# A two-layer fp32 kernel on one core: the first pair's projections as whole products, weight sums on VectorE, and a reordered layer 0 and tail

## The chip, the cores and the metric

The kernel runs on one core of one Trainium2 chip. Its engines run side by side, each in the order of its own queue, and wait for each other through semaphores: TensorE (PE: matrix products), VectorE (DVE), ScalarE (ACT), GpSimd (POOL) and SyncE (SP, which here only issues DMAs). The metric is the device time of one execution in microseconds (us), as the median of several runs. A profile is one further execution, recorded instruction by instruction.

## The reference, cut to what matters

Eight batches of 128 rows and 512 columns go through two layers, all in fp32. Both add their result to x.

```python
# layer 0: a per-batch 512x512 weight, then a feed-forward with 2 of 8 LoRA experts
c    = einsum('bsi,boi->bso', x, weight[adapter_ids])
wts  = softmax(top_k(einsum('bsd,ed->bse', c, gate_w), 2))
x    = x + einsum('bsd,od->bso', c, base_w) + base_b + 2 * lora(c, wts)
# layer 1: attention over a paged cache, then 16 of 64 small experts
q, k, v = x @ Wq.T, x @ Wk.T, x @ Wv.T        # 32 query heads, 8 key/value heads of 128
q, k = rope(rmsnorm(q)), rope(rmsnorm(k))
keys, values = concat(cache[pages], k), concat(cache[pages], v)     # 512 + 128 rows
o    = softmax(mask(q @ keys.T * SCALE)) @ values
x    = x + expert_ffn(o @ Wo.T)
```

## The kernel before, in words

Every instruction is placed by hand: the order of the calls in the program is the order of each engine's queue. Nothing is reordered by a scheduler. Tiles come from pools with a fixed number of buffers, and an instruction that writes a reused buffer waits until the old content has been read.

**Layer 0** (L347 to L626) loops over t = 0 to 7, one batch each. In one turn PE does: the first half of the adapter product (L470), the transpose of the low-rank values of batch t-1 (`ltp`, L528), the second half of the adapter, the experts' product of t-1 (`bp`, L534), the transposes of the finished rows of t-2 (`x1tp`, L553), then for batch t the gate and low-rank product (`gl`, L487, written into the adapter's bank `cp`) and the base product (L492). The adapter's result is copied to `cT` by DVE (L479). The top-2 choice is a chain of some dozen small DVE instructions in `l0_base` (L498 to L516), ended by `low`; one of them (L505) needs `lg`, whose upper part POOL fills with a large number, the sentinel (L497), and one (L510) needs an exponential from ACT (`ex`, L507). `l0_experts` adds up the row (L536), takes its largest value and a power of two from it (`up`, L540 to L545), ACT scales the row by it (L544), POOL forms `eps` (L546), and SP writes the row to memory. `l0_turn` then transposes it and ACT copies it to `xo` (L555), the input of layer 1.

**The projections** use a form of Strassen's and Winograd's scheme. Two batches form a pair. Both the pair's input and the weights are split into halves, and 7 products of half size (2 matmuls each) take the place of 8. `PRODUCTS` (L239) lists which sums of inputs and of weights each one multiplies; seven sums' places lie beside the data in `xo` (second index 0 to 6) and in the weight tile `wqkv` (likewise). The sums of the inputs (`sums_x`, 4 subtractions or additions of 256 columns) and of the weights (`sums_q`, 4 subtractions of 768 columns) are done on POOL. The results are put together by additions on DVE (L261), 7 for a pair and a weight tile. `project(k, j, products)` does the named products of pair k with weight tile j. Products 1, 3, 4 and 6 go to PSUM bank "q", and 2, 5 and 7 to bank "kv". In layer 0 `x1tp` uses bank "q" as well (for t-2 up to 5), and `ltp` uses bank "kv" (for t-1 up to 6).

**A unit** u is one batch with one key/value head (4 query heads): batch and head group follow from u, and 64 units make up layer 1. Pair 0 gives units 0 to 3, with weight tile 0 for units 0 and 2 and tile 1 for 1 and 3. `norms(u)` squares and sums the 5 heads on ACT and takes the root on POOL (`rs`, L295). `rotate(u)` applies the rotary embedding with 6 DVE instructions (L307 to L325; L321 needs `rs`) and leaves `ca`. Units 0 to 2 then have their heads transposed on PE (`transpose_qk`, `tq`, L339) and copied by ACT to `qkT`; later units go through an exchange by DMA (`blocks_qk`, `exchange_out`, `exchange_in`, `heads_qk`).

**The main loop** calls `iteration(u)` for u = 0 to 66. It runs, for each of 4 heads: two score products on PE (L768, L771); on DVE the scale, mask and smallest value (L781, giving `low`); the exponential on ACT (L792); the reciprocal of its sum on DVE (`den`, L797); the scaling on POOL (L798); and 32x32 block transposes on DVE (L803). Between the heads lie the output products of unit u-3 (L869) and the projections of a later pair (`slots`). At the end come norms and rotate for unit u+3 and the value products of unit u-2 (L847). Scores have two double banks, so the scores of head h+2 wait for L781 of head h. `gather` fetches 16 key pages of 32 KB for each batch through SP (`kt`), `gather_v` the values through POOL (`vt`).

The weight tiles live in two buffers. For each of the 3 later quarters of the heads they are loaded anew (`load_q`, 1.5 MB each, at the end of units 8 and 10, 24 and 26, 40 and 42), and their sums follow on POOL at the end of units 9 to 12, 25 to 28 and 41 to 44 (L1017).

Of the kernel before, what the change touches and what calls it, by code (L numbers as in the profile page):

```python
# [16 lines left out]
P = 128  # L17
B = 8
# [39 lines left out]
def adaln_ffn_kernel(  # L58
# [97 lines left out]

    def sums_q(g, first):

        w = wq_t[g]
        if first:  # L160
            nc.gpsimd.tensor_tensor(w[:, 5], w[:, 3], w[:, 1], ALU.subtract)
            nc.gpsimd.tensor_tensor(w[:, 1], w[:, 1], w[:, 0], ALU.subtract)
        else:
            nc.gpsimd.tensor_tensor(w[:, 4], w[:, 3], w[:, 1], ALU.subtract)
            nc.gpsimd.tensor_tensor(w[:, 6], w[:, 2], w[:, 4], ALU.subtract)

# [82 lines left out]
    def project(k, j, products):  # L249
# [3 lines left out]
        for i in products:  # L253
# [79 lines left out]

    def transpose_qk(u):
# [7 lines left out]
        qkT = pj.tile([P, NH, S], F32, tag="qkT", name=f"qkT_{u}", bufs=2)  # L342
        nc.scalar.copy(qkT.rearrange("p h s -> p (h s)"), t[:, : NH * S])
        qkT_t[u] = qkT


    with ExitStack() as l0:  # L347
# [35 lines left out]
        for b in (5, 6, 7):  # L383
            wt_home[b] = wp.tile([P, NC, DM], F32, tag="wo", name=f"wt_{b}", bufs=GH + 1)
        wt_home[4] = w0p.tile([P, NC, DM], F32, name="wt_4")
# [74 lines left out]

        state, cp_t, cT_t, lowT_t = {}, {}, {}, {}

        def l0_adapter(b, first):

            xT, wt, xb = loaded[b]
            if first:
                cp_t[b] = banks(f"cp_{b}")
            for o in range(0, NC // 2) if first else range(NC // 2, NC):
                for c in range(NC):
# [7 lines left out]
            if not first:  # L477
                cT_t[b] = p2.tile([P, NC, S], F32, tag="cT", name=f"cT_{b}")
                nc.vector.tensor_copy(cT_t[b].rearrange("p c s -> p (c s)"), cp_t[b][:, :DM])  # L479

        def l0_base(b):
# [13 lines left out]

            lg = sm.tile([P, E0 + 8], F32, tag="lg", name=f"lg_{b}")
            nc.gpsimd.memset(lg[:, E0:], BIG)  # L497
            nc.vector.tensor_copy(lg[:, :E0], gl[:, :E0])  # L498
# [62 lines left out]
        for t in range(B):  # L561
# [6 lines left out]
            if t + 2 < B:  # L568
                l0_load_x(t + 2)
            if t >= 1:  # L570
                l0_experts(t - 1)
                if t in (3, 4):
                    load_q(t - 3, nc.gpsimd)
            if 2 <= t <= 5:
# [6 lines left out]
            if t == 5:  # L581
                project(0, 0, (6, 7))
            if t == 6:
                project(0, 0, (3,))
                norms(0)
            if t == 7:
                project(0, 1, (6, 7))
            l0_base(t)
# [4 lines left out]
            if t in (3, 6):  # L593
                gather_v(t // 3 - 1, 0, LC)
            if t in (3, 5, 7):
                sums_x((t - 3) // 2)
            if t in (5, 7):
                make_tables(t // 7)
            if t in (4, 5):
                sums_q(t - 4, True)  # L600
                sums_q(t - 4, False)
            if t == 4:
                project(0, 0, (1, 2))
            if t == 5:
                project(0, 0, (4, 5))
            if t == 6:
                project(0, 1, (1, 2))
                rotate(0)
            if t == 7:
                transpose_qk(0)  # L610
                project(0, 1, (4, 5))
        for g in range(GH):
            load_o(g, nc.gpsimd)
        l0_turn_low(B - 1)
        project(0, 1, (3,))
        norms(1)
        l0_experts(B - 1)
        l0_turn(B - 2)
        rotate(1)
        norms(2)  # L620
        project(1, 0, (1, 2))
        l0_turn(B - 1)
        transpose_qk(1)
        rotate(2)
        project(1, 0, (6, 7))
        sums_x(B // 2 - 1)  # L626

# [103 lines left out]
    with ExitStack() as l1:  # L731
# [99 lines left out]
        def heads_qk(u):  # L831

            qkT = pj.tile([P, NH, S], F32, tag="qkT", name=f"qkT_{u}", bufs=2)
            nc.scalar.copy(
# [98 lines left out]
        def iteration(u):  # L933
# [76 lines left out]
            if on(u + 3):  # L1010
# [178 lines left out]
```

## Time and profile before

| what | value |
|---|---|
| median of 3 runs | 1287.82 us |
| lowest, highest | 1286.24, 1293.43 us |
| the profiled execution | 1288.46 us |
| its span, first to last instruction | 1286.7 us |
| PE busy | 1238.4 us, 96% of the span |
| DVE busy | 924.8 us, 72% |
| POOL busy | 609.3 us, 47% |
| ACT busy | 496.6 us, 39% |
| mean granted PE clock | 0.986 |
| first score product of unit 0 | 131.75 us after the start |
| first score product of unit 3 | 177.02 us |

In the views, a line of the list of instructions gives the start in us, the length, the engine, the source line, the operation, what it writes and reads, and in brackets how long the engine had been idle before it and what ended that idle time. A line of stages gives the stretch, its length, then the busy us of each engine with the number of instructions, the granted PE clock (1.00 is full), the share of the time in which the DMA engines were busy, and GB/s. An fp32 matmul stands as two records. PE runs faster than it looks busy: neighbouring records overlap a little, so lengths of work are best taken from start to start.

### The profile page before, as it was taken

Reading aid. Unit: us, or ns where it says so; the run is one execution under the profiler, and the core shown is the slowest. Engines: PE = TensorE matmul, PEld = TensorE weight load, DVE = VectorE, ACT = ScalarE, POOL = GpSimd, SP = SyncE. Lnnn points to the kernel's source line nnn. Section 1 sums busy time; section 2 is a strip of 40 time slices with the busy share of each in tenths; the row PEclk is TensorE's granted clock in tenths of the full one; section 3 lists DMA queues with packets and bytes.
Section 4 is the critical chain, followed back from the end, with each engine's and each line's share of the span. In section 5 each row is a group of like instructions: output and inputs, shape, how many; then the busy total and the mean of one; then the engine's idle time right before and its main releaser. Section 6 shows DMA issues by size and latency. Waiting matters only on the chain.

```text
span 1286.7 us, 15903 instructions
## 1 busy us (share of the span) xinstructions
PE 1238.4 (96%) x3835; PEld 654.1 (51%) x3835; DVE 924.8 (72%) x2049; ACT 496.6 (39%) x1437; POOL 609.3 (47%) x683
## 2 busy tenths in 40 slices
PE   9888899998999999999999999989999999999998
PEld 7655445554545545544455555544555555545544
DVE  3745887778987777778877777788877777767522
ACT  0222444433444444443444444343444444343210
POOL 2645454456654444456644444465544444443100
PEclk9989899999999999999999999999999999999999
DMA  8823287787887887788877877887878777887512
GB/s 292 277 68 110 86 240 243 246 257 245 263 260 234 266 248 252 246 278 265 276 243 246 275 242 247 281 261 251 273 245 266 244 236 245 272 250 233 181 65 89
DMA packets 211297, 298.99 MB, mean 232 GB/s; under 512 B 84035, under 2 KB 121284, under 8 KB 211204
## 3 DMA queue, kind: packets, MB, share of 16 engines
q1 hardware_dynamic: 180740, 207.83, 52.0%
q10 hardware_dynamic: 18960, 52.21, 12.2%
q0 software_dynamic: 11504, 37.94, 8.7%
q8 instruction: 31, 0.51, 0.2%
q14 instruction: 62, 0.51, 0.1%
HBM read 183.54 MB, written 114.36 MB: 232 GB/s over the span
## 4 chain that ended last, share of the span: by engine, by line
PE 68%; DVE 7%; DMA 6%; ACT 4%; POOL 2%; issue 2%; ACTq 0%; SPq 0%; DVEq 0%; POOLq 0%
PE p L258 16%; PE o L847 16%; PE y L869 14%; PE s L768 14%; PE s L771 4%; DMA px<-pb 3%; PE op L1086 2%; PE fz L680 2%; DMA qkb<-px 2%; ACT sq L289 2%; DVE ca L321 2%; DVE sa L321 2%; DMA kt<-in_kc 1%; POOL rs L295 1%; ACT p L792 1%
## 5 line engine op out<-in xcount | busy, mean ns | idle before, releaser
L798 POOL TENSOR_SCALAR p<-p,den 128x640 f32<-128x640 f32 x256 | 204.5, 799 | 438.0 <-DVE den L797 438.0
L792 ACT ACTIVATE p<-p,low 128x640 f32<-128x640 f32 x256 | 212.0, 828 | 461.3 <-DVE den L797 278.4
L258 PE MATMUL p<-wqkv,xo 128*128 128x384 f32 x896 | 327.2, 495 | 10.3 <-ACT xo L555 9.1
L781 DVE CUSTOM_DVE_ANT_0 p<-s,mask,rs 128x640 f32<-128x640 f32 x256 | 223.7, 879 | 115.3 <-PE s L771 112.6
L768 PE MATMUL s<-kt,qkT 128*128 128x512 f32 x512 | 267.1, 604 | 23.4 <-DVE low L781 16.5
L869 PE MATMUL y<-wo,oT 128*128 128x512 f32 x512 | 262.9, 598 | 3.2 <-ACT oT L858 3.2
L258 PEld LDWEIGHTS p<-wqkv,xo 128*128 128x128 f32 x896 | 172.4, 194 | 166.1 <-issue 81.6
L847 PE MATMUL o<-pT,vt 128*128 128x512 f32 x512 | 230.2, 592 | 0.0
L803 DVE STREAM_TRANSPOSE pb<-p 128x640 f32<-128x640 f32 x256 | 211.3, 825 | 16.2 <-POOL p L798 16.2
L771 PEld LDWEIGHTS s<-qkT 128*128 128x128 f32 x512 | 98.5, 192 | 124.8 <-issue 124.8
L768 PEld LDWEIGHTS s<-kt,qkT 128*128 128x128 f32 x512 | 96.2, 192 | 125.5 <-issue 53.6
L847 PEld LDWEIGHTS o<-pT,vt 128*128 128x128 f32 x512 | 97.3, 190 | 110.3 <-issue 94.9
L203 POOL DMA_INDIRECT vt<-in_vc,vrow x128 | 134.4, 1050 | 38.7 <-issue 28.0
L289 ACT ACTIVATE sq<-c 128x128 f32<-128x128 f32 x320 | 98.8, 309 | 10.5 <-DVE c L261 2.5
L295 POOL TENSOR_TENSOR rs<-ss,mhalf 128x5 f32<-128x5 f32 x64 | 98.1, 1533 | 5.3
L771 PE MATMUL s<-qkT 128*128 128x128 f32 x512 | 99.4, 276 | 0.0
L858 ACT COPY oT<-o 128x512 f32<-128x512 f32 x64 | 37.5, 586 | 138.5 <-PE o L847 133.9
L261 DVE TENSOR_TENSOR c<-c,p 128x384 f32<-128x384 f32 x96 | 51.9, 541 | 44.7 <-PE p L258 44.6
L869 PEld LDWEIGHTS y<-wo,oT 128*128 128x128 f32 x512 | 78.8, 193 | 8.6 <-issue 4.3
L321 DVE SCALAR_TENSOR_TENSOR ca<-c,rs,tab 128x128 f32<-128x128 f32 x64 | 42.6, 665 | 51.0 <-POOL rs L295 51.0
L847 PE MATMUL o<-pT,vn 128*128 128x512 f32 x128 | 65.4, 592 | 0.0
L289 ACT ACTIVATION_READ_ACCUMULATOR sq<-c 128x1 f32 x320 | 59.7, 187 | 0.0
(170 smaller groups left out, 1146.8 us busy)
## 6 DMA issues: line engine op xcount, KB each, us to landing
pT<-px SPq DMA_DIRECT2D x64, 1280.0 KB, 7.4
px<-pb SPq DMA_DIRECT2D x122, 400.0 KB, 5.4
px<-pb ACTq DMA_DIRECT2D x122, 400.0 KB, 5.2
qkb<-px SPq DMA_DIRECT2D x61, 320.0 KB, 3.5
kt<-in_kc SPq DMA_DIRECT2D x512, 32.0 KB, 4.7
wqkv<-in_wqkv POOLq DMA_DIRECT2D x8, 1536.0 KB, 11.4
wo<-in_wo POOLq DMA_DIRECT2D x8, 1024.0 KB, 7.5
yd<-ya SPq DMA_DIRECT2D x24, 256.0 KB, 2.0
```

The lines of the kernel that those rows point to most:

```text
L203: nc.gpsimd.indirect_dma_start(out=kv_t[step][1][:, c, :], out_offset=None, in_=vc, in_offset=bass.IndirectOffsetOnAxis(ap=vrow[:, hf, at ...
L258: nc.tensor.matmul(out=ps, lhsT=xo[:, pr, x, c, :], rhs=w[:, c, :], start=(c == 0), stop=(c == 1))
L289: nc.scalar.activation(sq, cs[:, at : at + D], AF.Square, accum_out=ss[:, h : h + 1])
L295: nc.gpsimd.tensor_tensor(rs, ss, mhalf, ALU.pow)
L768: nc.tensor.matmul(out=s[:, :L], lhsT=qkT[:, h, :], rhs=kt[:, :, g % GH, :], start=True, stop=True)
L771: nc.tensor.matmul(out=s[:, L:NK], lhsT=qkT[:, h, :], rhs=qkT[:, REP, :], start=True, stop=True)
L781: nc.vector.tensor_tensor_reduce(out=p, in0=s_t.pop((u, h))[:, :NK], in1=mask_t[st], scale=rs_t[u][:, h : h + 1], scalar=BIG, op0=ALU.add, ...
L792: nc.scalar.activation(p, p, AF.Exp, bias=low, scale=-1.0, accum_out=den)
L798: nc.gpsimd.tensor_scalar(p_t[u, h], p_t[u, h], den, 1.0, ALU.mult, ALU.mult)
L803: nc.vector.transpose(pb_t[u][:, :, h * w : (h + 1) * w].rearrange("p i (j a) -> p j i a", a=32), p_t.pop((u, h)).rearrange("p (j i a) -> ...
L847: nc.tensor.matmul(out=o, lhsT=vt[:, c, j * D : (j + 1) * D] if c < LC else vn_t.pop(u), rhs=pT[:, c], start=(c == 0), stop=(c == LC),)
L869: nc.tensor.matmul(out=y_t[st], lhsT=oT_t[u][:, h, :], rhs=wo_t[g][:, h, :], start=(h == 0 and j == 0), stop=(h == REP - 1 and j == GH - 1),)
```

## The change

1. **Pair 0 in whole products.** A new function `project_first(j, r, c)` computes one quarter of unit 2r+j directly: 4 matmuls of 384 columns that accumulate in one bank ("kv" for c = 1, "q" for c = 0), and one ACT copy. Eight calls, spread over t = 4 to 7 and the tail, take the place of the 14 products of `project(0, 0, ...)` and `project(0, 1, ...)`. They read only the plain halves of input and weights, so pair 0 needs no sums.
2. **Weight sums on DVE.** `sums_q(g, *tees)` does single named sums with `nc.vector`, 8 in layer 0, its tail and units 0 and 1, and 8 in each later reload: two inside head 1 of units 10 and 12 (mod 16), one at the end of these units, and one inside head 1 of units 11 and 13.
3. **Layer 0.** `cT` is copied by ACT. The `lg` tile and its sentinel come at the start of the turn. `l0_experts(t-1)` moves behind the gathers, `l0_turn(t-2)` and a projection.
4. **Tail.** norms and rotate of units 1 to 3 and the transposes of unit 2 are placed before the main loop; unit 2's heads go to the buffer of the last adapter weight. `sums_x` of pair 3 moves to unit 3, and that of pair 0 to unit 5.

```diff
+    def sums_q(g, *tees):
         w = wq_t[g]
-        if first:
-            nc.gpsimd.tensor_tensor(w[:, 5], w[:, 3], w[:, 1], ALU.subtract)
-            nc.gpsimd.tensor_tensor(w[:, 1], w[:, 1], w[:, 0], ALU.subtract)
-        else:
-            nc.gpsimd.tensor_tensor(w[:, 4], w[:, 3], w[:, 1], ALU.subtract)
-            nc.gpsimd.tensor_tensor(w[:, 6], w[:, 2], w[:, 4], ALU.subtract)
+        for t in tees:
+            to, x, y = {3: (5, 3, 1), 1: (1, 1, 0), 2: (4, 3, 1), 4: (6, 2, 4)}[t]
+            nc.vector.tensor_tensor(w[:, to], w[:, x], w[:, y], ALU.subtract)
...
+    def project_first(j, r, c):
+        u = 2 * r + j
+        if u not in c_t:
+            c_t[u] = pj.tile([P, 2 * HW], F32, tag=f"c{r}", name=f"c{r}_0_{j}", bufs=2)
+        ps = bank("kv" if c else "q", f"p_0_{j}_{r}{c}")[:, :HW]
+        for i in range(4):
+            x = i // 2
+            w = wq_t[j][:, 2 * x + c].rearrange("p (c n) -> p c n", c=2)
+            nc.tensor.matmul(out=ps, lhsT=xo[:, 0, 2 * r + x, i % 2, :], rhs=w[:, i % 2, :],
+                             start=(i == 0), stop=(i == 3))
+        nc.scalar.copy(c_t[u][:, c * HW : (c + 1) * HW], ps)
...
             if first:
                 cp_t[b] = banks(f"cp_{b}")
+                lg_t[b] = sm.tile([P, E0 + 8], F32, tag="lg", name=f"lg_{b}")
+                nc.gpsimd.memset(lg_t[b][:, E0:], BIG)
...
-                nc.vector.tensor_copy(cT_t[b].rearrange("p c s -> p (c s)"), cp_t[b][:, :DM])
+                nc.scalar.copy(cT_t[b].rearrange("p c s -> p (c s)"), cp_t[b][:, :DM])
...
-            if t >= 1:
-                l0_experts(t - 1)
-                if t in (3, 4):
-                    load_q(t - 3, nc.gpsimd)
+            if t in (3, 4):
+                load_q(t - 3, nc.gpsimd)
...
             if t == 5:
-                project(0, 0, (6, 7))
+                project_first(0, 0, 1)
+                norms(0)
             if t == 6:
-                project(0, 0, (3,))
-                norms(0)
+                project_first(0, 1, 0)
             if t == 7:
-                project(0, 1, (6, 7))
+                project_first(1, 1, 1)
+                transpose_qk(0)
+            if t >= 1:
+                l0_experts(t - 1)
             l0_base(t)
...
-            if t in (3, 5, 7):
-                sums_x((t - 3) // 2)
             if t in (5, 7):
+                sums_x(t // 2 - 1)
                 make_tables(t // 7)
-            if t in (4, 5):
-                sums_q(t - 4, True)
-                sums_q(t - 4, False)
             if t == 4:
-                project(0, 0, (1, 2))
+                project_first(0, 0, 0)
             if t == 5:
-                project(0, 0, (4, 5))
+                project_first(0, 1, 1)
+                sums_q(0, 3, 1)
             if t == 6:
-                project(0, 1, (1, 2))
+                project_first(1, 0, 1)
                 rotate(0)
+                norms(2)
+                sums_q(0, 2, 4)
             if t == 7:
-                transpose_qk(0)
-                project(0, 1, (4, 5))
+                project_first(1, 0, 0)
+                norms(1)
+                sums_q(1, 3, 1)
         for g in range(GH):
             load_o(g, nc.gpsimd)
         l0_turn_low(B - 1)
-        project(0, 1, (3,))
-        norms(1)
-        l0_experts(B - 1)
+        project_first(1, 1, 0)
         l0_turn(B - 2)
         rotate(1)
-        norms(2)
+        l0_experts(B - 1)
         project(1, 0, (1, 2))
+        transpose_qk(1)
+        norms(3)
+        rotate(2)
         l0_turn(B - 1)
-        transpose_qk(1)
-        rotate(2)
         project(1, 0, (6, 7))
-        sums_x(B // 2 - 1)
+        transpose_qk(2, wt_7.rearrange("p c n -> p (c n)")[:, : NH * S])
+        rotate(3)
...
                     if h > 0:
                         normalize(u, h - 1)
+                    if h == 1:
+                        reload = (u // 16 + 1) * GH + u % 16 // 12
+                        if u == 1:
+                            sums_q(1, 4)
+                        elif u % 16 in (10, 12) and u < NU - 8:
+                            sums_q(reload, 3, 1)
+                        elif u % 16 in (11, 13) and u < NU - 8:
+                            sums_q(reload, 4)
...
                 heads_qk(u + 1)
+            if u == 0:
+                sums_q(1, 2)
+            elif u % 16 in (10, 12) and u < NU - 8:
+                sums_q(reload, 2)
...
-            if u == 0:
-                transpose_qk(2)
-            if on(u + 3):
+            if 3 < u + 3 < NU:
                 norms(u + 3)
...
-            if u > 8 and u < NU - 8 and u % 16 in (9, 10, 11, 12):
-                sums_q((u // 16 + 1) * GH + u % 16 // 11, u % 16 in (9, 11))
+            if u in (3, 5):
+                sums_x(3 if u == 3 else 0)
```

More of the change, by code (lines that the diff above doesn't have):

```diff
@@ L155, in load_q @@
         wq_t[g] = t
-    def sums_q(g, first):
+    def sums_q(g, *tees):
         w = wq_t[g]
-        if first:
-            nc.gpsimd.tensor_tensor(w[:, 5], w[:, 3], w[:, 1], ALU.subtract)
-            nc.gpsimd.tensor_tensor(w[:, 1], w[:, 1], w[:, 0], ALU.subtract)
-        else:
-            nc.gpsimd.tensor_tensor(w[:, 4], w[:, 3], w[:, 1], ALU.subtract)
-            nc.gpsimd.tensor_tensor(w[:, 6], w[:, 2], w[:, 4], ALU.subtract)
+        for t in tees:
+            to, x, y = {3: (5, 3, 1), 1: (1, 1, 0), 2: (4, 3, 1), 4: (6, 2, 4)}[t]
+            nc.vector.tensor_tensor(w[:, to], w[:, x], w[:, y], ALU.subtract)
     def sums_x(pr):
@@ L280, in project @@
                 add(c0[:, HW:], c0[:, HW:])
+    def project_first(j, r, c):
[6 more added lines that the diff above has]
+            w = wq_t[j][:, 2 * x + c].rearrange("p (c n) -> p c n", c=2)
+            nc.tensor.matmul(
+                out=ps,
+                lhsT=xo[:, 0, 2 * r + x, i % 2, :],
+                rhs=w[:, i % 2, :],
+                start=(i == 0),
+                stop=(i == 3),
+            )
+        nc.scalar.copy(c_t[u][:, c * HW : (c + 1) * HW], ps)
     def norms(u):
@@ L332, in adaln_ffn_kernel, with transpose_qk @@
     qkT_t = {}
-    def transpose_qk(u):
+    def transpose_qk(u, home=None):
         qk = qk_t.pop(u)
@@ L341, in transpose_qk @@
             )
-        qkT = pj.tile([P, NH, S], F32, tag="qkT", name=f"qkT_{u}", bufs=2)
-        nc.scalar.copy(qkT.rearrange("p h s -> p (h s)"), t[:, : NH * S])
-        qkT_t[u] = qkT
+        if home is None:
+            home = pj.tile([P, NH * S], F32, tag="qkT", name=f"qkT_{u}", bufs=2)
+        nc.scalar.copy(home, t[:, : NH * S])
+        qkT_t[u] = home.rearrange("p (h s) -> p h s", h=NH)
     with ExitStack() as l0:
@@ L383, in adaln_ffn_kernel @@
         for b in (5, 6, 7):
-            wt_home[b] = wp.tile([P, NC, DM], F32, tag="wo", name=f"wt_{b}", bufs=GH + 1)
+            wt_7 = wp.tile([P, NC, DM], F32, tag="wo", name=f"wt_{b}", bufs=GH + 1)
+            wt_home[b] = wt_7
         wt_home[4] = w0p.tile([P, NC, DM], F32, name="wt_4")
@@ L459, in l0_angles @@
                 nc.scalar.activation(cos, kk, AF.Sin, bias=half_pi, scale=-1.0)
-        state, cp_t, cT_t, lowT_t = {}, {}, {}, {}
+        state, cp_t, cT_t, lowT_t, lg_t = {}, {}, {}, {}, {}
         def l0_adapter(b, first):
@@ L494, in l0_base @@
                 )
-            lg = sm.tile([P, E0 + 8], F32, tag="lg", name=f"lg_{b}")
-            nc.gpsimd.memset(lg[:, E0:], BIG)
+            lg = lg_t.pop(b)
             nc.vector.tensor_copy(lg[:, :E0], gl[:, :E0])
@@ L831, in heads_qk @@
         def heads_qk(u):
-            qkT = pj.tile([P, NH, S], F32, tag="qkT", name=f"qkT_{u}", bufs=2)
+            qkT = pj.tile([P, NH * S], F32, tag="qkT", name=f"qkT_{u}", bufs=2)
+            qkT = qkT.rearrange("p (h s) -> p h s", h=NH)
             nc.scalar.copy(
@@ L1009, in iteration @@
                 exchange_out(u)
-            if on(u + 3):
+            if 3 < u + 3 < NU:
                 rotate(u + 3)
```

## The prediction, made before the changed kernel ran

> **What bounds the kernel now.** I read first the page's busy shares (PE 96%, DVE 72%, ACT 39%, POOL 47% of the span), so time can only come from PE's idle and its slow clock. Then the list of what PE waited for, over the run and over the first 177 us:
>
> ```profile
> PE s L768 <- DVE low L781: 16.5, 11, 4.7
> PE p L258 <- ACT xo L555: 9.1, 3, 3.1
> PE s L768 <- DMA kt<-in_kc: 3.8, 3, 1.9
> PE ltp L528 <- DVE c L261: 3.8, 1, 3.8
> PE y L869 <- ACT oT L858: 3.2, 4, 2.3
> ...
> PE s L768 <- DVE low L781: 8.3, 3, 4.7
> ```
>
> The reader is to see: total us, times, longest. The last line is the first 177 us alone. Half of the waits for `low`, and all of the two that name xo and c, lie before unit 3; the other 8.2 us for `low` come later. Third, PE's stages there (busy PE, PEld, DVE, ACT, POOL, then PE clock, DMA share, GB/s), cut at t=5, t=6, t=7, the tail, units 0, 1, 2:
>
> ```profile
> 57.87:84.28 26.41, 19.55 (x72) 13.10 (x71) 14.12 (x29) 3.05 (x5) 19.51 (x17) 0.81 0.39 133
> 84.28:100.74 16.46, 13.48 (x69) 9.21 (x67) 7.69 (x23) 4.33 (x16) 4.43 (x7) 1.00 0.24 64
> 100.74:120.52 19.78, 16.71 (x77) 11.16 (x76) 9.46 (x29) 2.45 (x5) 10.30 (x14) 0.91 0.42 126
> 120.52:131.75 11.23, 9.46 (x38) 5.55 (x37) 8.91 (x19) 7.32 (x28) 5.33 (x7) 1.00 0.28 94
> 131.75:142.32 10.57, 9.27 (x34) 5.18 (x33) 10.13 (x23) 3.08 (x7) 3.57 (x6) 1.00 0.02 5
> 142.32:159.61 17.29, 12.55 (x34) 6.75 (x33) 13.14 (x28) 7.66 (x26) 6.91 (x9) 0.80 0.48 152
> 159.61:177.02 17.41, 14.44 (x39) 7.30 (x38) 15.57 (x34) 8.16 (x29) 8.61 (x10) 0.90 0.71 224
> ```
>
> Fourth, the time-ordered list of instructions, for what ends each wait:
>
> ```profile
> 57.15 1.82 POOL L161 TENSOR_TENSOR wqkv<-wqkv 128x768 f32<-128x768 f32 x1
> 56.01 0.09 DVE L505 MATCH_VALUE_LOAD rep<-top,lg 128x8 f32 x1 [2.62 <-POOL lg L497]
> 63.60 0.33 PE L528 MATMUL ltp<-ident,low 128*128 128x128 f32 x1 [3.78 <-DVE c L261]
> 71.73 5.46 PE L258 MATMUL p<-wqkv,xo 128*128 128x384 f32 x8 [3.08 <-ACT xo L555]
> 150.82 2.08 PE L768 MATMUL s<-kt,qkT 128*128 128x512 f32 x2 [4.74 <-DVE low L781]
> 277.00 0.35 DVE L321 SCALAR_TENSOR_TENSOR ca<-c,rs,tab 128x128 f32<-128x128 f32 x1 [0.49 <-POOL rs L295]
> 314.33 2.96 DVE L321 SCALAR_TENSOR_TENSOR ca<-c,rs,tab 128x128 f32<-128x128 f32 x1 [0.50 <-POOL rs L295]
> 315.31 1.82 POOL L164 TENSOR_TENSOR wqkv<-wqkv 128x768 f32<-128x768 f32 x1
> 320.96 1.13 PE L768 MATMUL s<-kt,qkT 128*128 128x512 f32 x2 [1.87 <-DVE low L781]
> ```
>
> While POOL forms weight sums, a DVE instruction of 0.35 us takes 2.96 us, and PE then waits 1.87 us. Early, the same sums and the late sentinel hold DVE, which holds the bank of ltp.
>
> [...] The trace agrees (0.35 against 1.90 to 2.96 us for L321 beside 1.80 us sums). [...] rows agree at N=512 (691 ns, L443) and 320 (493 ns, L324). So I price a 768-column sum on DVE, which no row shows, at an estimated 0.957 us against 1.80 on POOL. [...] here the pair of s matmuls after 4.74 us idle took 2.08 instead of 1.02 us, after 0.72 us idle nothing was lost.
>
> **The change, part by part.** PE pieces, start to start at full clock from that list: adapter halves 1.78 each, ltp 0.11, experts matmul 0.86, turn 0.43, gl 0.93, bp 3.44, so 9.33 us for one t; a product (2 matmuls) 1.29; a 5-transpose 0.54.
>
> *Products.* 14 products become 8 projections of 4 matmuls: 8 x 2.58 - 14 x 1.29 = +2.6 us of PE. 14 additions on DVE (0.55 each, 7.7 us) go; ACT copies of 0.47 us go from 2 to 8 for the pair (+2.8 us) and stand in ACT's idle time (3.05 of 26.41 us busy at t=5). ACT also takes cT (0.69 us on DVE, about 0.57 as the xo copy of the same shape).
>
> *Loss of each stage now* (length minus pure work): t=5 26.41-14.49=11.9; t=6 16.46-13.2=3.3; t=7 19.78-15.03=4.8; tail 11.23-8.82=2.4; unit 0 10.57-8.73=1.8; unit 1 17.29-9.48=7.8; unit 2 17.41-12.5=4.9; t=4 0.3. Sum 37.2 us.
>
> *Loss that I expect there after.* I walk the new order queue by queue, from 45.7 us (t=4), where nothing before it changes.
> - t=5: the sentinel is written an iteration's head earlier, POOL has no sums, and the turn's copy no longer follows L544's wait for `up` on ACT. Low of t is ready about 5.2 us after the experts matmul (31.83 to 36.77 now); PE has 0.93+3.44+2.58+1.78=8.7 us of work before it needs it. At t=1 to 3 there is no projection and the turn no longer covers it: 6.15 against 5.2. No loss, 1 us of cover.
> - t=6: project_first(0,1,0) writes bank q, which the turn's copy has just to empty; ACT does cT first: 0.57+0.57 after the second half, minus the turn's 0.43: 0.9 us lost. t=7 uses kv: 0. The norms(2) put ahead of lowT(6) on ACT (5 x 0.43 + 0.39 = 2.5, after a 0.5 copy that starts at 87.5) end near 90.5, lowT and cT near 91.4, and PE is at its next use of them at 94.8: covered.
> - POOL's four x sums and two table products at t=5 and t=7 (about 4.4 us) now fall beside DVE's base chain and two weight sums[...]. I add 1.8 us to low and 0.5 per sum: within cover at t=5, about even at t=7.
> - Tail: 45.7+11.9 (t=4)+14.5+14.5+0.9+15.0: the last projection of t=7 ends near 102.6. ACT copy 0.5, squares 2.2, POOL 1.6, rotate_k 1.5 on DVE, 0.4 of hand-overs: ca(1) at 108.8, 1 us before PE arrives. x1(7) is queued behind rotate(1) on DVE, then L544 on ACT: x1tp(7) starts 111.5, 1.1 us late; rotate(2) then ends 115.6, tq(2) 1 us late. s of unit 0 starts near 116.2 (now 131.75): 13.6 us for 10.65 of work, 3.0 lost.
> - rotate(3) and the mask follow on DVE: first L781 at 119.9 (now 135.98). Units 0 to 2 are bound by DVE: unit 0 now takes 8.85 us from its first L781 to its last transpose; plus one sum, without rotate(3): unit 1 at 129.8 (now 149.88). Unit 1 has a sum too but less wait: unit 2 at 144.6 (now 165.26). From there PE needs 11 to 12 us with its clock loss to unit 3, near 156.9 (now 177.02). Pure work 30.2, 10.6 lost.
> - qkT(3) needs the exchange of unit 1: 11.2 us from last transpose to landing now, so ready 153.3: not last, by 3 us.
> Sum lost after: 0.9+3.0+10.6=14.5. Early gain 37.2-14.5-2.6 = 20.1 us. Bounds: every wait closed to the last as long as the covers named hold gives 24; x1(7) late by 3 more us and each unit by 1.5 gives 12.
>
> *Reloads* (units 9 to 13, 25 to 29, 41 to 45). Waits for `low` there: 1.87+0.83, 0.39+1.25+0.82, 0.37+1.87+0.83 = 8.2 us, and 1.7 us of slow clock after 865.03. Each follows a stretched L321 pair. After, DVE loses the stretches (about 3.1+4.2+3.1+3.1=13.5 us a set) and gains 8 sums, 7.7 us: two at h=1 in a 1.4 us gap[...], one at the end, one at h=1. Behind them stand the addition of the product, L781 and the transposes; the slip of 1 to 2 us is under the 2.3 us by which L781 of head 0 leads PE's third s now. The exchange and load_q also slip by about 1 us, so the kt gathers do (3.8 us of waits that stay, and may take back some). Of 9.9 us I take 7.5; bounds 1 and 10. The other sums leave POOL free where it wasn't late.
>
> *The rest.* sums_x(3) and (0) at units 3 and 5 put 2.9 us of POOL after rs, beside rotate: up to 2.5 us on DVE under 3 us of lead: 0, if uncovered 1. Moved DMAs: load_q(0) and (1) earlier by some us, SP's gathers ahead of x1_d's write; the bus is 0.2 to 0.4 busy after 58 us: nothing.
>
> Total 20.1+7.5=27.6. The profiled execution took 1288.46 (span 1286.7); the median is 1287.82. 1288.46-27.6=1260.9; I say 1261.
>
> **The rivals.**
> 1. Reload part lost: with `low` on time, the kt gathers and sums on DVE end last. For: three waits already name kt; DMA share is 1.0 for 12 to 20 us after each load_q. Against: at 328 to 332 us it had fallen to 0.57, before the next s. 1288.5-20.1-1 = 1267.
> 2. Early chain not shortened in the tail: x1(7) behind rotate(1), norms ahead of lowT on ACT, units still at DVE's pace. Only t=5 to t=7 and part of the units gain: 1288.5-12-7.5 = 1269.
> 3. Slower: cT on ACT closes a ring. ACT runs in order; if ex(t), waiting on DVE, or norms hold lowT and cT of the next t, gl waits each t. It decides from 27.6/7 = 4 us late in each turn, where the whole gain is gone; at 5 us: 1261+35 = 1296. Against: ACT is 6.08 of 45.70 us busy at the start and ex is ready 4 us before lowT.
> 4. The change does nothing, as other waits replace all: 1287.
>
> **How the numbers follow.** Forecast 0.57 (own range 1255 to 1266), rival 1 0.17, rival 2 0.19, rival 3 0.03, rival 4 0.04. The range 1252 to 1274 takes the bounds of both terms (24+10 down, 12+1 up), leaving rivals 3 and 4 and a little out. Half a per cent (6.4 us) is about what a measurement of this kernel tells from no change: faster 0.93, same 0.04, slower 0.03.
>
> **What would show it.** Right: in PE's waits the xo and c entries are gone or under 1 us each; first L781 near 120, unit 3 near 157; L321 never above 1 us in the reloads, and s<-low waits there under 0.5. Wrong: a wait of PE for lowT, cT or ca(2) above 2 us, L162 on DVE at 1.5 us or more each, or kt waits above 6 us in sum.

## The result, and the profile after

The changed kernel took **1267.03 us** (median of 4 runs, 1266.13 to 1272.15) against 1287.42 us for the kernel before on the same chip: ratio 0.9845, 95% interval 0.9809 to 0.9881, so faster by 1.6%, or 20.4 us. The forecast of 1261 lies 6 us below it. The profiled execution took 1267.55 us; its span is 1265.6 us, 21.1 less than the span before.

In the changed kernel line numbers shift: the score product is L787, its mask and minimum L800, `ca` with rs L336, the projection matmuls L255 and (whole products) L288, the weight sum on VectorE L162, the copy of the exchanged heads `qkT` L854, `pb` from the heads L773.

What PE waited for, over the whole run of the changed kernel (total us, times, longest):

```profile
PE s L787 <- ACT oT L878: 7.2, 5, 1.7
PE s L787 <- DVE low L800: 4.4, 3, 2.2
PE y L889 <- ACT oT L878: 3.7, 5, 2.4
PE s L787 <- DMA kt<-in_kc: 3.7, 2, 2.0
PE s L787 <- DMA px<-pb: 3.4, 2, 2.1
PE p L255 <- DVE c L258: 2.2, 1, 2.2
PE x1tp L571 <- ACT xb L562: 1.5, 1, 1.5
```

The waits for xo and c in layer 0 are gone from the head of this list, and `low` fell from 16.5 to 4.4 us, all before unit 3. The first, fourth and fifth lines are 14.3 us, all before the first score of a unit: 10, 12, 14, 26, 28, 30, 42, 44 and 46. Lines of this kind stood in the kernel before too: `kt` had 3.8 us, and `px` had a line that the prediction's list left out:

```profile
PE s L768 <- DMA px<-pb: 3.1, 2, 2.3
```

Of these 6.9 us, 0.8 belong to unit 20 and 6.1 to units 10, 26, 28 and 42. With the 8.2 us for `low`, PE waited 14.3 us before scores in the reloads, and it waits 14.3 us now: the names changed, the sum did not. `oT` and `px` are no inputs of a score, so something else came last.

The seven early stages of the changed kernel (t=5, 6, 7, the tail, units 0, 1, 2; columns as in the prediction):

```profile
57.21:71.70 14.49, 14.49 (x72) 9.98 (x71) 4.93 (x19) 6.80 (x19) 4.55 (x7) 1.00 0.58 199
71.70:87.19 15.49, 14.77 (x72) 10.01 (x71) 7.97 (x24) 3.21 (x7) 8.01 (x9) 1.00 0.29 80
87.19:102.24 15.05, 15.05 (x78) 10.44 (x76) 8.80 (x25) 6.10 (x19) 8.14 (x11) 1.00 0.17 50
102.24:116.08 13.84, 11.39 (x47) 6.80 (x45) 11.00 (x23) 8.31 (x30) 8.18 (x10) 1.00 0.49 155
116.08:125.52 9.44, 8.47 (x31) 4.62 (x30) 9.10 (x23) 3.35 (x7) 2.22 (x3) 1.00 0.20 53
125.52:140.31 14.79, 11.35 (x34) 5.93 (x33) 12.08 (x29) 5.76 (x16) 6.11 (x8) 0.91 0.49 161
140.31:157.25 16.94, 14.76 (x39) 7.40 (x38) 15.03 (x32) 7.70 (x27) 8.64 (x10) 0.88 0.78 246
```

In t=5 and t=7 PE is busy for the whole stage (14.49 of 14.49 and 15.05 of 15.05). Unit 3 starts at 157.25 instead of 177.02: **19.8 of the 21.1 us are gained by there**, and only 1.3 from unit 3 to the end.

Where the rest of the forecast went is read from the time between the first score products of neighbouring units. Undisturbed, an odd unit follows after 15.92 us and an even one after 17.21 (units 5 to 9 do so exactly, before and after). What units 10 to 15, 26 to 31 and 42 to 47 take beyond that, in us (rounded after adding), for each kernel of this study that bears on it:

| kernel | 1st reload | 2nd | 3rd | sum |
|---|---|---|---|---|
| before | 7.6 | 6.2 | 7.8 | 21.6 |
| changed | 6.7 | 7.6 | 6.4 | 20.7 |
| e1: changed, reloads' sums on GpSimd | 8.5 | 6.2 | 6.5 | 21.3 |
| e2: K pages twelve and four | 9.1 | 12.1 | 11.9 | 33.1 |
| e5: no weight transfers | 1.7 | 0.7 | 0.7 | 3.2 |
| e6: no weight transfers, sums on GpSimd | 2.5 | 2.5 | 2.5 | 7.4 |
| e7: transfers in halves | 5.7 | 5.8 | 4.3 | 15.9 |
| e9: halves, and Wo moved | 3.4 | 2.7 | 2.9 | 9.0 |

Between these two executions the change took 0.9 us out of 21.6. The table has one execution of each kernel, and the sum scatters: four more kernels with the changed reload code (e8, e10, e11 and e12 below) have 22.6, 24.7, 24.3 and 19.5 us. So 0.9 cannot be told from nothing; but the 14 us that a gain of 7.5 would have left is far below all five. The time-ordered list of the changed kernel shows what the waits are now, around the start of unit 10:

```profile
256.48 1.71 SPq L834 DMA_DIRECT2D px<-pb  x2
258.06 1.02 POOL L151 DMA_DIRECT2D wqkv<-in_wqkv  x1
258.12 0.35 DVE L336 SCALAR_TENSOR_TENSOR ca<-c,rs,tab 128x128 f32<-128x128 f32 x1 [0.49 <-POOL rs L310]
272.20 0.72 ACT L854 COPY qkT<-qkb 128x640 f32<-128x640 f32 x1 [2.73 <-DMA qkb<-px]
276.61 1.10 PE L787 MATMUL s<-kt,qkT 128*128 128x512 f32 x2 [1.35 <-DMA px<-pb]
276.65 0.35 DVE L336 SCALAR_TENSOR_TENSOR ca<-c,rs,tab 128x128 f32<-128x128 f32 x1 [2.91 <-POOL rs L310]
```

L336 itself is short now, 0.35 us as foreseen. But the 1.5 MB weight transfer is issued at 258.06, and the exchanged heads `qkb` land so late that ACT idles 2.73 us before their copy. The squares of the next norm stand behind that copy on ACT, rs behind them on POOL, so L336 waits 2.91 us where it waits 0.49 in a plain unit, and the next L800 comes late with it. PE's score waits besides, for 1.35 us. Nearly the same happens at 307.72 and 312.40 and at 342.29 and 347.64.

The DMA engines in these microseconds, changed kernel, stretches of 4 us (the last two columns are DMA share, which can read slightly above 1 in this view, and GB/s):

```profile
258.00:262.00 4.00, 3.93 (x13) 2.02 (x12) 3.21 (x9) 1.51 (x3) 3.36 (x5) 1.00 1.02 333
262.00:266.00 4.00, 4.00 (x14) 2.17 (x13) 1.74 (x6) 2.08 (x4) 2.69 (x4) 1.00 0.95 293
266.00:270.00 4.00, 4.00 (x14) 2.25 (x13) 3.20 (x8) 1.16 (x4) 1.00 (x2) 1.00 1.06 351
270.00:274.00 4.00, 4.00 (x11) 1.92 (x11) 3.56 (x7) 1.74 (x7) 0.80 (x1) 1.00 1.03 343
274.00:278.00 4.00, 2.65 (x8) 1.09 (x7) 1.31 (x4) 1.78 (x8) 2.63 (x3) 1.00 0.97 222
```

They are full for the whole unit: a share of 0.95 to 1.06 in each stretch.

### The profile page after: what moved, and what is told of

It reads as the page before. It is cut to its first block, busy times and chain, and to the rows that moved or that the text cites. A ratio compares the mean times of both kernels' runs of the same rounds, so it can differ in the third digit from the quotient of the medians.

```text
span 1265.6 us, 15910 instructions
## 1 busy us (share of the span) xinstructions
PE 1230.3 (97%) x3843; PEld 650.5 (51%) x3843; DVE 901.1 (71%) x2059; ACT 507.1 (40%) x1451; POOL 559.4 (44%) x651
## 4 chain that ended last, share of the span: by engine, by line
PE 72%; DMA 12%; DVE 6%; issue 3%; POOL 3%; ACT 2%; SPq 1%; ACTq 1%; DVEq 0%; POOLq 0%
PE p L255 15%; PE o L867 15%; PE y L889 15%; PE s L787 14%; DMA px<-pb 5%; DMA pT<-px 4%; PE s L790 4%; PE op L1116 2%; PE fz L699 2%; DVE pb L822 2%; PE cp L489 2%; DMA kt<-in_kc 2%; DVE wqkv L162 2%; PE bp L511 1%; DVE c L258 1%
## 5 line engine op out<-in xcount | busy, mean ns | idle before, releaser
L817 POOL TENSOR_SCALAR p<-p,den 128x640 f32<-128x640 f32 x256 | 209.6, 819 | 459.5 <-DVE den L816 459.5
L800 DVE CUSTOM_DVE_ANT_0 p<-s,mask,rs 128x640 f32<-128x640 f32 x256 | 224.6, 879 | 128.2 <-PE s L790 125.5
L255 PE MATMUL p<-wqkv,xo 128*128 128x384 f32 x840 | 303.0, 490 | 2.2 <-DVE c L258 2.2
L787 PE MATMUL s<-kt,qkT 128*128 128x512 f32 x504 | 259.6, 597 | 16.5 <-ACT oT L878 7.2
L255 PEld LDWEIGHTS p<-wqkv,xo 128*128 128x128 f32 x840 | 159.5, 191 | 147.9 <-issue 76.5
L787 PEld LDWEIGHTS s<-kt,qkT 128*128 128x128 f32 x504 | 95.1, 191 | 115.5 <-issue 50.8
L258 DVE TENSOR_TENSOR c<-c,p 128x384 f32<-128x384 f32 x90 | 48.5, 539 | 33.2 <-PE p L255 33.2
L336 DVE SCALAR_TENSOR_TENSOR ca<-c,rs,tab 128x128 f32<-128x128 f32 x64 | 23.4, 365 | 56.8 <-POOL rs L310 56.8
## 6 DMA issues: line engine op xcount, KB each, us to landing
wqkv<-in_wqkv POOLq DMA_DIRECT2D x8, 1536.0 KB, 12.1
```

What stands on the lines that cost most here:

```text
L255: nc.tensor.matmul(out=ps, lhsT=xo[:, pr, x, c, :], rhs=w[:, c, :], start=(c == 0), stop=(c == 1))
L787: nc.tensor.matmul(out=s[:, :L], lhsT=qkT[:, h, :], rhs=kt[:, :, g % GH, :], start=True, stop=True)
L800: nc.vector.tensor_tensor_reduce(out=p, in0=s_t.pop((u, h))[:, :NK], in1=mask_t[st], scale=rs_t[u][:, h : h + 1], scalar=BIG, op0=ALU.add, ...
L817: nc.gpsimd.tensor_scalar(p_t[u, h], p_t[u, h], den, 1.0, ALU.mult, ALU.mult)
```

## The experiments

Twelve kernels ran. Each ratio is to the kernel before, run on the same chip, with its 95% interval. Two kernels with the same reload code can differ by some us: the third reload alone took 10.7 us beyond plain in e11 and 6.4 in the changed kernel, whose early parts differ but whose reloads do not. So medians a few us apart are not told apart here, and the traces decide.

### e1: the reloads' sums back on GpSimd

```diff
-                        elif u % 16 in (10, 12) and u < NU - 8:
-                            sums_q(reload, 3, 1)
...
+            if u > 8 and u < NU - 8 and u % 16 in (9, 10, 11, 12):
+                sums_pool((u // 16 + 1) * GH + u % 16 // 11, u % 16 in (9, 11))
```

> The changed kernel with only the reloads' twelve weight sums back on GpSimd, in pairs at the ends of units 9 to 12 of each sixteen; the early part stays changed. Theory A (in a reload the K gather of the next step lands last, behind the weight load, so the sums' engine hardly matters): 1268 us, at most 3 us above the changed kernel's 1267.0; the first score of units 10, 12 and 14 still waits 1 to 2 us, and the score after a stalled ca/sa of unit 11 waits again. Rival B (the sums on VectorE did save the forecast 7.5 us and something else lost as much): 1274 to 1275 us. Rival C (the sums on VectorE are themselves what delays the first scores of units 10, 12 and 14): faster than the changed kernel by 2 us or more, and those waits fall below 0.5 us.

Measured: 1266.0 us, ratio 0.9834 (0.9809 to 0.9858): no different from the changed kernel. The stretched instruction is back in its time-ordered list (there L342), and yet the kernel is no slower:

```profile
276.45 1.90 DVE L342 SCALAR_TENSOR_TENSOR ca<-c,rs,tab 128x128 f32<-128x128 f32 x1 [3.11 <-POOL rs L316]
293.94 2.96 DVE L342 SCALAR_TENSOR_TENSOR ca<-c,rs,tab 128x128 f32<-128x128 f32 x1 [0.50 <-POOL rs L316]
```

PE's waits for low rise from 4.4 to 13.8 us, while the waits before scores that name kt, px and oT fall from 14.3 to 5.7. The two sums are 18.7 and 19.5 us. So the reload part of the change is worth nothing measurable, and rival B is out. Rival C is out by the time here, and more clearly by e5 below.

### e2, e3, e4: gather the K pages earlier

The gather of the next step's K pages was my first suspect. Twelve of 16 pages were moved to the even unit:

```diff
-            first = u % GH * NPP // GH
+            first, end = (0, 12) if u % GH == 0 else (12, NPP)
             if pages:
                 gather(st + 1, first, first + 3)
...
-                gather(st + 1, first + 3, first + NPP // GH)
+                gather(st + 1, first + 3, end)
```

> The changed kernel with twelve of a step's sixteen K pages gathered in the even unit and four in the odd one, instead of eight and eight; nothing else moved. Theory A (the last K pages, issued in the odd unit behind a 1.5 MB weight load, are what the first score of the next even unit waits for): those nine waits of 1.3 to 2.1 us go[...]; 12 to 18 us less than the changed kernel, 1249 to 1255 us. Rival C (VectorE's sums, or the exchange of the probabilities, are late and not the gather): within 1.5 us of 1267, the waits stay. Rival D (the transfers only change places: another of the same units' transfers becomes late): 1260 to 1265, with waits at other places in units 9 to 14.

> Both edits at once: the reloads' sums on GpSimd and the K pages gathered twelve and four. Theory A: with the gather out of the way the sums' engine shows its price: 3 to 8 us above the kernel with the gather alone moved, with waits of the reloads' ca/sa and low again. If the sums' engine never mattered: within 1 us of it.

> The kernel before with the K pages gathered twelve and four. Theory A: the kernel before lost part of its reloads to the same late gather: 8 to 14 us less than its 1287.4, about 1276 us, and the first scores of units 26, 28 and 42 no longer wait for kt. If its reload losses came from GpSimd's sums alone: within 2 us of 1287.4.

Measured: e2 1290.8 us (0.9998 to 1.0036), e3 1293.3 (1.0032 to 1.0066), e4 1308.9 (1.0132 to 1.0188). The edit costs 21 to 27 us in each kernel, so all three expectations failed (e3's 2.5 us above e2 tells nothing beside that). By the table 12.4 us of e2's loss lie in the reloads' units. Another 13 lie elsewhere, most of it at units 18 to 24, 32 to 40 and 48 to 52, where the other transfers of Wo run (issued at the ends of units 17, 33 and 49). In the list of DVE's waits of e2 a line of 3.2 us in the changed kernel became

```profile
DVE pb L773 <- DMA px<-pb: 62.0, 21, 7.3
```

and its time-ordered list shows how, for unit 9:

```profile
248.85 8.57 SPq L190 DMA_DIRECT2D kt<-in_kc  x9
257.52 0.69 SPq L913 DMA_DIRECT2D yd<-ya  x1
258.30 2.85 SPq L834 DMA_DIRECT2D px<-pb  x2
271.69 0.85 DVE L773 STREAM_TRANSPOSE pb<-ca 128x640 f32<-128x640 f32 x1 [6.49 <-DMA px<-pb]
273.75 2.35 PE L255 MATMUL p<-wqkv,xo 128*128 128x384 f32 x4 [4.18 <-DVE c L258]
```

Nine page gathers hold SP's queue for 8.57 us. SP issues `px` behind them at 258.30 to 261.15 instead of 256.48 to 258.19, now at and after the weight transfer, not ahead of it. There is one buffer for `pb`, so DVE waits 6.49 us to refill it and PE waits for DVE. The gather can't be treated as free to move: SP's queue, the one `pb` buffer and the weight transfer form a ring. Whether the K pages are late in the changed kernel is not settled by this, since the edit made other work late; their landings are read below. The transfers as a whole were tested next.

### e5 and e6: without the weight transfers

```diff
     def load_q(g, eng):
 
+        if g >= GH:
+            wq_t[g] = wq_t[g - GH]
+            return
...
     def load_o(g, eng):
+        if g >= GH:
+            wo_t[g] = wo_t[g - GH]
+            return
```

> The changed kernel without the twelve weight transfers of the three reloads: every later pair of groups uses the first pair's Wq/Wk/Wv and Wo, so the projections and the output of six of eight groups are of other weights; sums, matmuls and all other transfers stay. Theory A2 (a reload's waits all come from the 1.5 MB transfer filling the DMA engines, whatever its sums do): the waits of the first scores of units 10, 12 and 14 fall below 0.3 us; of the 20.7 us by which the reloads' units exceed the plain ones at least 15 go: 1247 to 1252 us. Rival C (VectorE's sums delay those scores): the waits stay near 1 us or more, 1262 to 1267.

> The same without the transfers, with the reloads' sums on GpSimd in pairs as in the kernel before (later groups use the first pair's weights, as there). The price of the sums' engine with nothing else late: the forecast's 7.5 us (ca/sa waiting for rs behind two sums, low late after it) says 7 to 8 us above the kernel without transfers and sums on VectorE; if the transfers were also what made GpSimd's sums late, 1 to 4 us above it.

Six of the eight groups then work with the wrong weights, so these two kernels leave out a part of the computation and serve for timing alone. Measured: e5 1249.2 us, ratio 0.9701 (0.9668 to 0.9735), e6 1251.8 us, ratio 0.9732 (0.9702 to 0.9762). Taking away the twelve transfers removes 17.5 of the 20.7 us, and PE's waits before scores in the reloads are gone, though VectorE still forms the sums there. In e5's time-ordered list ACT's copy and the next L342 are on time:

```profile
268.47 0.71 ACT L860 COPY qkT<-qkb 128x640 f32<-128x640 f32 x1
273.33 0.35 DVE L342 SCALAR_TENSOR_TENSOR ca<-c,rs,tab 128x128 f32<-128x128 f32 x1 [0.49 <-POOL rs L316]
```

With GpSimd's sums and no transfers (e6) the sums show their own price:

```profile
272.83 1.91 DVE L348 SCALAR_TENSOR_TENSOR ca<-c,rs,tab 128x128 f32<-128x128 f32 x1 [0.49 <-POOL rs L322]
295.89 1.12 PE L799 MATMUL s<-kt,qkT 128*128 128x512 f32 x2 [0.82 <-DVE low L812]
```

By the table that is 4.3 us a run (7.44 - 3.16), 2.6 by the medians (whose intervals overlap). Beside the transfers it is 21.3 - 20.7 = 0.6, which the scatter hides.

### e7 and e9: halves, and Wo elsewhere

```diff
-                load_q((k // 4 + 1) * GH + j, nc.gpsimd)
+                load_q((k // 4 + 1) * GH + j, nc.gpsimd, 0, 2)
+            if u % 16 in (9, 11) and u < NU - 8:
+                load_q((u // 16 + 1) * GH + u % 16 // 11, nc.gpsimd, 2, 4)
```

The two last arguments are the slices of the weight tile that are loaded. The sums move on by half a unit. e9 adds one line:

```diff
-            if u % 16 == 12 and u < NU - 16:
+            if u % 16 == 5 and u < NU - 16:
                 load_o((u // 16 + 1) * GH, nc.gpsimd)
```

> The changed kernel with each reload of Wq/Wk/Wv cut into halves of 0.75 MB, issued at the ends of units 8 and 9 (second group 10 and 11) instead of one of 1.5 MB at the end of unit 8 (10), and its four sums half a unit later. Theory A2 (the burst of one unit is what makes its exchange and gathers late): each unit's DMA load fits into its 16 us, the waits at units 10 and 12 fall below 0.7 us: 8 to 14 us less than the changed kernel, 1253 to 1259 us. If the total and not the burst decides: 1264 to 1268, the waits spread over units 10 to 13.

> The kernel with split weight loads, and besides the 1 MB Wo transfer of the reload's first group issued at the end of the fifth unit of each sixteen instead of the twelfth, next to the Wq/Wk/Wv halves; its buffer is free since the second. In the kernel with split loads units 14, 30 and 46 still began 3.4, 4.4 and 2.9 us late, behind that transfer. Theory A2 (bursts): these fall below 1 us and nothing appears at units 6 and 7: 6 to 10 us less than the split kernel's 1259.0, 1249 to 1253 us. If a megabyte costs the same wherever it goes: 1257 to 1260, with new waits at units 6 to 8.

Measured: e7 1259.0 us, ratio 0.9785 (0.9752 to 0.9817); e9 **1254.1 us** (5 runs), ratio 0.9738 (0.9717 to 0.9760). e9 is faster than both kernels: its interval lies below that of the changed kernel. It missed its expected window by 1 us. In e7 one large wait remained at units 14, 30 and 46:

```profile
345.68 1.10 PE L787 MATMUL s<-kt,qkT 128*128 128x512 f32 x2 [1.85 <-DMA px<-pb]
```

In e9 it is gone, units 6 to 8 are as before, and what remains is small and behind `oT`:

```profile
268.23 0.71 ACT L854 COPY qkT<-qkb 128x640 f32<-128x640 f32 x1
273.10 0.35 DVE L336 SCALAR_TENSOR_TENSOR ca<-c,rs,tab 128x128 f32<-128x128 f32 x1 [0.49 <-POOL rs L310]
292.19 1.13 PE L889 MATMUL y<-wo,oT 128*128 128x512 f32 x2 [1.08 <-ACT oT L878]
```

The same bytes moved at other times cost 11.7 us less (20.7 against 9.0): the burst decides, not the total. e7 also moves the sums, but e9 differs from e7 by the one transfer alone, and 6.9 of the 11.7 us are its.

### e8 and e12: what carries the early gain

e8 puts the first two groups' sums back on GpSimd, in place:

```diff
-            nc.vector.tensor_tensor(w[:, to], w[:, x], w[:, y], ALU.subtract)
+            eng = nc.gpsimd if g < GH else nc.vector
+            eng.tensor_tensor(w[:, to], w[:, x], w[:, y], ALU.subtract)
```

> The changed kernel with the eight weight sums of the first two groups back on GpSimd, at the places where VectorE has them now; the eight whole products, the copies on ScalarE and the order stay. If the early gain comes from the whole products needing no sum (the forecast): 0 to 3 us above 1267, the last projection of the eighth stage at 102 to 103.5 us. If it comes from taking the sums off GpSimd: 5 us or more above, with waits for xb, eps or rs in stages 5 to 7.

e12 undoes the whole products and keeps the sums on VectorE:

```diff
             if t == 5:
-                project_first(0, 0, 1)
-                norms(0)
+                project(0, 0, (6, 7))
...
+            if t in (4, 5):
+                sums_q(t - 4, 3, 1, 2, 4)
             if t == 4:
-                project_first(0, 0, 0)
+                project(0, 0, (1, 2))
...
-        project_first(1, 1, 0)
+        project(0, 1, (3,))
+        norms(1)
...
```

> The changed kernel with the first pair again projected as fourteen products with additions, in the order of the kernel before, but with its eight weight sums on VectorE (four each at the ends of stages 4 and 5), and the first sum of x at stage 3; the copies, the sentinel, the order of the turns and the tail stay changed. If the whole products carry the early gain (the forecast's step: no additions, no sums needed before the tail, for 2.6 us more of TensorE): 5 to 12 us above 1267.0, with TensorE waiting for c or low's bank in stages 5 to 7 again. If taking the sums off GpSimd was enough and the whole products brought nothing: 1263 to 1267.

Measured: e8 1272.8 us, ratio 0.9904 (0.9869 to 0.9939), first score of unit 0 at 119.13 instead of 116.08 and of unit 4 at 178.73 instead of 175.36, 3.1 and 3.4 us late; of unit 3 at 158.85, 1.6 us late. e12 1277.6 us, ratio 0.9944 (0.9926 to 0.9963), unit 0 at 125.05 (9.0 us late), unit 3 at 163.43 (6.2 us late). e12's median lies in the window of the whole products. e8's lies 5.7 us above the changed kernel's, in the window of the sums' engine, but its trace does not bear that out: stages t=5 and t=6 last 14.49 and 15.49 us as in the changed kernel, and the loss begins in the tail. e8's time-ordered list there:

```profile
106.30 3.68 POOL L163 TENSOR_TENSOR wqkv<-wqkv 128x768 f32<-128x768 f32 x2
106.36 1.89 DVE L337 SCALAR_TENSOR_TENSOR ca<-c,rs,tab 128x128 f32<-128x128 f32 x1 [1.98 <-POOL rs L311]
111.11 0.77 PE L355 MATMUL tq<-ident,ca 128*128 128x128 f32 x5 [1.83 <-DVE ca L341]
```

The L321 stall of the reloads in small: two sums on POOL, a rotation held beside them, PE waiting for its result. Here no late transfer hides it. e12's list at t=6:

```profile
72.71 5.50 DVE L162 TENSOR_TENSOR wqkv<-wqkv 128x768 f32<-128x768 f32 x4
79.85 0.48 PE L546 MATMUL ltp<-ident,low 128*128 128x128 f32 x1 [4.03 <-DVE c L258]
```

Four sums in a row hold DVE 5.50 us ahead of the additions, an addition holds the bank that ltp needs, and PE waits 4.03 us: the wait of 3.78 us that the prediction showed at t=5, one stage later. So the products' additions and their need of early sums are worth 6 to 9 us, and the sums' engine, once the whole products leave room for late sums, 2 to 3. Part of e12's loss is the place of its sums, which the 14 products force.

### e10 and e11: the tail, and the copies and sentinels

```diff
-        norms(3)
         rotate(2)
         l0_turn(B - 1)
         project(1, 0, (6, 7))
-        transpose_qk(2, wt_7.rearrange("p c n -> p (c n)")[:, : NH * S])
-        rotate(3)
...
+            if u == 0:
+                transpose_qk(2)
-            if 3 < u + 3 < NU:
+            if on(u + 3):
                 norms(u + 3)
...
```

> The changed kernel with the work of units 2 and 3 back where it was: the norms and the rotation of unit 3 and the turn of unit 2's heads in unit 0, not in layer 0's tail. If the tail's rearrangement is a part of the gain of its own (about 3 us of VectorE work taken out of unit 0, which VectorE bounds): 3 to 6 us above 1267.0, unit 0 longer by that and unit 3's first score at 160 us or later. If the early gain lies in stages 5 to 7 alone: within 1.5 us of 1267.

```diff
-                nc.scalar.copy(cT_t[b].rearrange("p c s -> p (c s)"), cp_t[b][:, :DM])
+                nc.vector.tensor_copy(cT_t[b].rearrange("p c s -> p (c s)"), cp_t[b][:, :DM])
...
-            lg = lg_t.pop(b)
+            lg = sm.tile([P, E0 + 8], F32, tag="lg", name=f"lg_{b}")
+            nc.gpsimd.memset(lg[:, E0:], BIG)
```

> The changed kernel with cT's copy back on VectorE and the sentinel of lg back behind the products of its stage, the rest as changed. If the ring over low, lg and cT was closed by GpSimd's sums alone (the forecast's step for the fifth stage: the cover is then 8.7 us for 5.2): 0 to 3 us above 1267.0. If the copy and the sentinel hold the ring by themselves: 8 us or more above it, with PE waiting for cT, lowT or low's bank by 1 us or more in stages 5 to 7.

Measured: e10 1269.8 us, ratio 0.9882 (0.9849 to 0.9914); e11 1270.3 us, ratio 0.9850 (0.9814 to 0.9886). e10 came between its two windows, e11 0.2 us above its first. By the traces taking back either part alone loses nothing early. In e10 unit 0 starts at 114.44, 1.6 us earlier than in the changed kernel, and then the list of PE's waits before unit 3 has the old one again:

```profile
PE s L784 <- DVE low L797: 8.2, 3, 4.7
```

Unit 3 starts at 157.60 against 157.25: a rotation on VectorE costs the same in the tail as in unit 0. In e11 unit 0 starts at 115.95 and unit 3 at 157.00. With the new products and sums the copy and the sentinel do not close the ring; what they would do with the old ones, no run shows. The two medians are 3 us above the changed kernel's, with overlapping intervals, and the traces put this into later stages.

Taken together: at the first score of unit 0 the change has gained 15.7 us, of which e12 gives back 9.0 and e8 3.1, e10 and e11 nothing. At unit 3 it has gained 19.8, of which they give back 6.2 and 1.6. No run undoes two parts at once, or the new order of `l0_experts` and `l0_turn`, so what carries the other 12 us at unit 3 is not shown.

## Why the prediction came out as it did

- **t=5 to t=7: right.** Forecast losses 0, 0.9 and 0; measured against the same pure work 14.49-14.49 = 0, 15.49-14.49 = 1.0 (the wait for xo at bank q, 0.72 us, where it was put) and 15.05-15.03 = 0. The last projection of t=7 ended at 102.2 (forecast 102.6). That the whole products carry a good part is shown (e12); that the rest is as the step put it, is argued. The covers for lowT and cT held: PE's largest wait for cT is 0.7 us. The 1.8 us on low and the 0.5 us per sum that the step adds at t=5 and t=7 were its author's estimate. Measured, two sums beside GpSimd's x sums took 2.75 us at 70.97 and again at 101.01, and two at 88.34, beside the issue of a `vt` gather, 1.94 us: 0.4 us more per sum. What low lost was not measured apart.
- **Tail: right.** x1tp(7) started at 111.79, late by 1.54 (forecast 111.5 and 1.1), unit 0 at 116.08 (116.2).
- **Units 0 to 2: right in sum, with one wait not foreseen.** First L800 of units 0, 1, 2 at 119.72, 129.44, 145.48 (119.9, 129.8, 144.6), unit 3 at 157.25 (156.9). In unit 1 the one `pb` buffer was not free, by the time-ordered list of the changed kernel:

```profile
135.52 0.84 DVE L773 STREAM_TRANSPOSE pb<-ca 128x640 f32<-128x640 f32 x1 [2.17 <-DMA px<-pb]
137.59 1.65 PE L255 MATMUL p<-wqkv,xo 128*128 128x384 f32 x2 [2.23 <-DVE c L258]
```

  Unit 0's exchange had not left it. The step named the additions and transposes behind the sum, not the buffer. Unit 2's first L800 is 0.9 us later than forecast; the wait is long enough for that. A second buffer would take 12.8 KB of each partition (3200 columns of 4 bytes); it was not tried.
- **Early gain: 19.8 us measured, 20.1 forecast.**
- **Reloads: the step that failed is "Of 9.9 us I take 7.5".** It measured 0.9, which the scatter does not tell from nothing. The mechanism in it happened: no L336 is stretched (0.35 us at most in the reloads, and PE has no wait for `low` there), and the sums on DVE took 0.93 to 1.52 us each. The mis-sized term is what PE gets of it. The step counted waits by the name at their end and took the DMA waits as a separate 3.8 us, without the 3.1 us that name `px`. But the two kinds stood in line in each reload: a stalled unit 11 gave the transfers time. ACT's copy of the exchanged heads before unit 10 and before unit 12, in the kernel before, and before unit 12 in the changed one:

```profile
290.68 0.72 ACT L834 COPY qkT<-qkb 128x640 f32<-128x640 f32 x1 [2.66 <-DMA qkb<-px]
327.39 0.71 ACT L834 COPY qkT<-qkb 128x640 f32<-128x640 f32 x1
307.72 0.72 ACT L854 COPY qkT<-qkb 128x640 f32<-128x640 f32 x1 [3.16 <-DMA qkb<-px]
```

  Before, the transfers were late for unit 10 and no longer for unit 12, whose last K page landed 1.8 us before its first score; after, they are late for both. Also the 7.5 us was too much for GpSimd's sums by themselves: with no transfers they cost 4.3 (e6 against e5).
- **The rest.** sums_x at unit 3 was put at 0, if uncovered at 1: in the profiled execution unit 3 took 18.11 instead of 17.21 us, 0.9, though not in every other kernel with the same line. From unit 4 to the end the changed kernel gains 0.9 in the reloads, 1.6 at unit 20, which was late before and is not after (luck: e11, with the changed code there, is late by 1.5 again), and 0.1 at the end, and loses 0.4 at unit 36. With the 0.9 lost at unit 3 that is the 1.3 us.
- **Rival 1 came true**, with its time of 1267: DMAs ended last. Its other half, sums on VectorE ending last, did not: e5 keeps these sums, and the waits are gone. It named kt, and the landings in the trace agree. The last K page for unit 10 was issued at 270.43 and took 5.9 us to land, about 0.2 us before the score at 276.61, while qkT was ready at 272.92. So it is at units 14, 28, 30, 44 and 46: the last page lands 0.2 us before the score, after 5.1 to 6.1 us, and qkT is ready 3.7 us or more before. (At the undisturbed unit 20 the last page takes 2.9 us.) For units 12, 26 and 42 the trace has no landing of the last page. That the weight transfers make them late is shown (e5, e7, e9). Against this rival the prediction held that the DMA share had fallen to 0.57 at 328 to 332 us. That stretch followed a stalled unit; in the changed kernel the units are shorter and the share stays near 1 to the next score (0.99 to 1.06 from 294 to 310 us, then 0.90 up to the score at 312.40).
- **Its signs.** "kt waits above 6 us in sum" was to show it wrong. The line that names kt has 3.7 us, and the sign was missed by name but not in substance: at six of the nine scores behind these three lines of 14.3 us, the landings above put a K page last. L162 on DVE took

```profile
L162 DVE TENSOR_TENSOR wqkv<-wqkv x32: 934/1126/1517, 71.0 to 877.3; 128x768 f32<-128x768 f32 x32
```

  (min, median, max in ns, by the view of one line): the estimate of 957 ns lies near its floor and 15% under its median. A straight line through the prediction's two rows, 493 ns at 320 columns and 691 at 512, gives 955 at 768.

In the changed kernel's trace, from 260 to 268 us, while the weight transfer ran, the row of GpSimd's transfers (weights and values) moved 406 packets with 1.69 MB and the row of SP's 419 with 0.41 MB: nearly one for one, with packets of four times the size on GpSimd's side. qkb, in SP's row, landed 8.2 us after its issue in unit 9, and 3.4 us after it in unit 10, beside no weight transfer.

## What to carry to other kernels

Before pricing a wait, ask what would have been late if it had not been there: here the stall of unit 11 gave the transfers time (the last K page for unit 12 landed 1.8 us before its score), and removing it renamed the wait (14.3 us before scores in the reloads, before and after). A sum over waits by name was here an upper bound at best (8.2 us by name, 0.9 us gained); run the stage without the suspected transfers, and once more with the old stall, to get the price of each alone and together. Where the DMA share was near 1 (0.95 to 1.06), moving bytes to stages with room was worth 13 us here (two edits, e9), and moving the sums between engines nothing that could be measured.

## What the hardware showed

- A 0.35 us DVE instruction took 1.89 to 2.96 us beside GpSimd's 1.8 us sums again in e1, e6 and e8. The 2.96 us (e1 at 293.94, the kernel before at 314.33) lie beside two GpSimd instructions in a row: the issue of a weight transfer (1.01 us, from 293.87 and 314.27) and the first sum after it. On DVE, the same sums took 0.93 to 1.52 us.
- Gathering four more K pages early, with no byte more, cost 21 to 27 us. In unit 9 nine small issues held SP's queue for 8.57 us (0.95 us each, against 0.33 us for the shortest), and the exchange was issued at and after a 1.5 MB transfer, not before it. About half of e2's loss lies outside the reloads and is not explained here.
- Outside the reloads, units 4 to 59 of e5 keep their spacing of 15.92 and 17.21 us to within 0.02 us, so every late unit is seen at once by the first score's time.
- Beside a weight transfer the DMA engines moved nearly one packet of GpSimd's row for each of SP's (406 against 419 in 8 us). A last K page of 32 KB took 2.9 us to land at the quiet unit 20 and 5.1 to 6.1 us in the reloads.
